# Four graph layers on one core: the adjacency test moved to the front, the first graphs listed anew, and seeds in place of a search

## The chip, the core and the metric

The kernel runs on one of the eight cores of a Trainium2 chip. The metric is the device time of one execution in microseconds. The time before is the median of three runs; one more execution was recorded by the hardware profiler, and the profile tells of that one.

## What is computed

There are 32 graphs of 512 nodes with 128 features in float32, and one adjacency matrix `adj` (512 x 512, zeros and ones, about 1.6% ones) that all graphs share. Four layers follow each other; each adds to `x` what it computes from `h = relu(layernorm(x))`:

```python
# layer 0
x_h = elu(h @ Wi + bi)
e = sigmoid(a_tgt[:, :, None] + a_src[:, None, :] + be) * (adj + 0.005 * (1 - (adj != 0)))
recv = elu(concat([einsum('bij,bjh->bih', e, x_h), x_h * sum(e, -1)]) @ Wn + bn)
x += concat([recv, x_h]) @ Wm + bm
# layer 1: five steps of a gated unit; m = adj @ h stands for both message inputs
z, r = sigmoid(m @ w3 + ... + h @ u3), sigmoid(m @ w4 + ... + h @ u3)
h = (1 - z) * h + z * tanh(m @ w5 + ... + (r * h) @ u5)
# layer 2
x += adj @ (h @ W) + bias
# layer 3: h, adj @ h, adj^2 @ h and adj^3 @ h (the two adjacencies are the same), each times a weight
```

## The kernel before

**Tiles.** A graph is one tile of 128 partitions by 512. Four graphs share a group buffer `x`. All other values live in numbered buffers: 36 of kind `f` (128x512 float32 in SBUF), 8 banks of PSUM of kind `b`, small ones for statistics (`s`), DRAM scratch (`m`, `d`). Layers 1 to 3 multiply by the adjacency in a rounded float32 type with a high and a low part (`r`), against the transposed adjacency (`A_r`), its column-shuffled form (`AQ`) and its square (`AA`).

**Order of the work.** No loop runs on the chip. Python code declares every operation with an engine, an estimated duration, a due time and its operands (`op`, line 63). The class `Plan` then plays the operations against those durations and writes one fixed order of instructions for each engine (`order`, line 124): of the operations that are ready, the one with the smallest due time goes first. An operation marked `two` excludes another such operation at the same time; by default all of GpSimd's operations are marked, and the VectorE operations with two inputs in SBUF. Where the plan finds TensorE without work before its time `FILL` (50), it inserts a matmul of ones into a spare bank, whose result nobody reads (line 348). The chip's engines run their lists in order and wait for each other by semaphores; the planned times are not on the chip.

**Two arms.** The kernel does not assume that the adjacency holds only zeros and ones. VectorE counts the other entries (line 561), TensorE sums the counts (line 582), VectorE writes the number to `other` (line 587), and every engine reads it and branches (lines 1069 and 1070). The arm `binary`, which these inputs take, uses the rounded type; the other arm is in float32. The part before the branch is planned up to time `BRANCH` (18), and each arm from there. Instructions that are listed later than that time stand behind the branch on their engine. For the arm `binary`, the function `searched_order` (line 221) shifts due times at random while the kernel is built, 240 times, and keeps the order whose planned end is earliest.

**The start.** SP issues the loads: `x` of graphs 0 and 1, the weight `Wi` and bias, the four blocks of `adj` (`A_nat`), `x` of graph 2, further weights. TensorE transposes the adjacency (line 570); ACT copies the result to `A_r` (line 572) and scales it by 200 (line 574), and VectorE makes from both the mask (1 where the entry is 0, 200 where it is 1; line 575). GpSimd copies the untransposed blocks to the rounded type (line 849) for the square.

**The layers' lines.** Layernorm (line 515): statistics on VectorE (lines 524 to 527), the power -1/2 on GpSimd (line 529), a shift on VectorE (line 533), then scale, shift and Relu on ACT (line 538); for the first `FIRST` (2) graphs the normalisation is on VectorE instead (line 544), the Relu is in the copy after the transpose (line 615), and the Relu of the first elu is on VectorE (line 600 in place of 603). Layer 0: projection (line 492, used for all products with one weight), scores (lines 634 to 641), tanh of the pair sums (line 686), times the mask (line 689), aggregation (line 697), row sums (lines 705 and 714, from graph 3 on by accumulating DMAs of GpSimd, line 721), output (line 744). Layer 1: adjacency products (line 913), rounding (lines 883 and 887), copies (lines 481 and 925). Graphs from the third on are turned by VectorE's 32x32 transpose and two DMAs through DRAM (line 433 and its DMAs at lines 435 to 474). Layer 3: lines 988 and 997, and the result at line 1015. Weights of the later layers are loaded behind the branch, summed on VectorE (line 800) and transposed (line 802).

Of the kernel before, what the change touches and what calls it, by code (L numbers as in the profile page):

```python
# [17 lines left out]
P = 128  # L18
# [4 lines left out]

class Val:
# [11 lines left out]
class Op:  # L36
    def __init__(self, eng, us, result, emit, two, keep):
        self.eng, self.us, self.result, self.emit, self.two, self.keep = eng, us, result, emit, two, keep
        self.before, self.after, self.vals, self.takes = set(), [], [], []
        self.ready, self.begun = 0.0, False  # L40


class Plan:
# [7 lines left out]
    def __init__(self, slots, ahead, last):  # L51
        self.ahead, self.last, self.ops, self.vals = ahead, last, [], {}
        self.free = {k: [(0.0, i) for i in range(n)] for k, n in slots.items()}
        self.until = dict.fromkeys(self.RESULT, 0.0)
        self.shared, self.now = 0.0, 0.0
        self.careful = 0.0
        self.slack = 0.0
        self.pieces = {}
        self.cold = 4.5
        self.fill = 0.0  # L60
        self.idle = None

# [61 lines left out]
    def order(self, end=None):  # L124

        left = [o for o in self.ops if not o.begun]
        for o in reversed(left):
            o.chain = o.us + max([o.margin, *(o.result + a.chain for a in o.after)])
            if end is None:
                o.due = min(o.due, self.last - o.chain)  # L130
        by_due, oldest = sorted(left, key=lambda o: o.due), 0
# [14 lines left out]
        def begins(o, now):  # L146
            if o.due > by_due[oldest].due + self.ahead:
                return False
            if o.two and self.shared > now:
                return False  # L150
            keep = 0 if o is by_due[oldest] else o.keep
            if any(v.added and self.clean(now) is None for v in o.takes):
                return False
            return all(
                len(self.free[v.kind]) > keep and self.free[v.kind][keep][0] <= now
                for v in o.takes
            )

        while events:
# [3 lines left out]
            for e in self.until:  # L163
                while coming[e] and coming[e][0][0] <= now:
                    _, i, o = heapq.heappop(coming[e])
                    heapq.heappush(ready[e], (o.due, i, o))
# [11 lines left out]
                if o is not None and now < self.careful and any(  # L178
                    c.due < o.due and t < now + 0.3 * o.us for t, _, c in coming[e]
                ):  # L180
                    heapq.heappush(ready[e], (o.due, index[o], o))
                    o = None
# [9 lines left out]
                while oldest + 1 < len(by_due) and by_due[oldest].begun:  # L192
                    oldest += 1
# [27 lines left out]
    def searched_order(self, until, rounds):  # L221


        ops = [o for o in self.ops if not o.begun]
        early, rng, asked = [o for o in ops if o.due < until], random.Random(3), self.state()

        def listed(due):
            self.back_to(asked)
            for o, d in zip(early, due):
                o.due = d  # L230
            return self.order()

        best, first = None, [o.due for o in early]
        due = first
        for _ in range(rounds):
            try:
                listed(due)
                end = max(o.start + o.us for o in ops)
                if best is None or end <= best[0]:
                    best = end, due  # L240
            except AssertionError:
                pass
            due = [*best[1]]
            if rng.random() < 0.5:
                start, width = rng.uniform(15, until), rng.uniform(2, 15)
                shift, eng = rng.gauss(0, 4), rng.choice(["PE", "ACT", "DVE", None, None])
                varied = {i: shift for i, o in enumerate(early)
                          if start <= first[i] < start + width and eng in (None, o.eng)}
            else:
                n = max(1, int(len(early) * rng.uniform(0.01, 0.1)))  # L250
                varied = {i: rng.gauss(0, 4) for i in rng.sample(range(len(early)), n)}
            for i, shift in varied.items():
                due[i] += shift
        return listed(best[1])


@with_exitstack
def tile_four_graph_layers(
# [35 lines left out]
    PACE, FIRST_PACE, LAST_PACE = 56.0, 14.0, 30.0  # L294
    BRANCH, FILL = 18.0, 50.0
    MARGIN = 10.0
    FIRST = 2

    T_MM, T_TR, T_NARROW, T_PASS = 0.86, 0.44, 0.224, 0.23
    T_VEC, T_COPY, T_ACT, T_DMA = 0.61, 0.5, 0.6, 0.45  # L300
# [82 lines left out]
    load_graph(0, -9, 2.5)  # L383
    load_graph(1, -9, 2.9)
    Wi_sb = load_const(Wi, [P, P], "Wi_sb", -9)
    bi_sb = load_column(bi, "bi_sb", -9)
    A_nat = [Val("f") for _ in range(NC)]
    for v in A_nat:
        v.left += 1
    for ic in range(NC):  # L390
        load(A_nat[ic], adj[ts(ic, P), :], -8, 0.48, result=3.9 + 0.2 * ic)
    load_graph(2, -8, 4.8)
# [12 lines left out]
    def scaled(v, factor, name, due):  # L405
        t = const(name, [P, 1])
        op("POOL", 0.4, due, lambda: nc.gpsimd.tensor_scalar(
            at(t), at(v), factor, None, op0=ALU.mult), [v], [t])
        return t
# [105 lines left out]
    def layernorm(b, due, relu=True, earliest=0.0):  # L515
# [6 lines left out]
        def moments():  # L522
# [5 lines left out]
        op("DVE", 1.3, due, moments, [X[b]], [s], earliest=earliest)  # L528
        op("POOL", 1.35, due, lambda: nc.gpsimd.tensor_tensor(  # L529
            stat(SCALE), stat(VAR), at(neg_half), op=ALU.pow), [s, neg_half], [s])  # L530
# [16 lines left out]
        if relu:  # L547
            op("ACT", 1.56, due, scale, [X[b], s], [h])
        else:
            op("DVE", 0.9, due, normed, [X[b], s], [h])  # L550
# [5 lines left out]
    A_r, mask = const("A_r", [P, NC, N], F32R), const("mask", [P, NC, N])  # L556
    other = const("other", [1, 1], I32)
    n_odd = const("n_odd", [P, NC])
    for ic in range(NC):
        odd = Val("f")  # L560
        op("DVE", 0.7, 9, lambda ic=ic, odd=odd: nc.vector.scalar_tensor_tensor(
# [3 lines left out]
    for jc in range(NC):  # L565
        pt, z = Val("b"), Val("f")
        pt.pieces = True
        def turn(jc=jc, pt=pt):
# [3 lines left out]
        op("ACT", T_COPY, 22, lambda jc=jc, pt=pt: nc.scalar.copy(at(A_r)[:, jc, :], at(pt)),  # L572
           [pt], [A_r])
        op("ACT", T_COPY, 9 + jc, lambda z=z, pt=pt: nc.scalar.mul(at(z), at(pt), 1 / ALPHA), [pt], [z])
        op("DVE", T_VEC, 9 + jc, lambda jc=jc, z=z, pt=pt: nc.vector.scalar_tensor_tensor(
            at(mask)[:, jc, :], at(pt), 0.0, at(z), op0=ALU.is_equal, op1=ALU.add),
            [pt, z], [mask])
# [8 lines left out]
    op("PE", 0.3, 9, count, [n_odd, ones], [p_odd])  # L586
    op("DVE", 0.2, 9, lambda: nc.vector.tensor_copy(at(other), at(p_odd)[:1, :1]),
# [23 lines left out]
    def layer0(b, h, due):  # L611
        KEEP = 12
        if b < G:
            pt, hT = transposed(h, due), Val("f")
            op("ACT", T_COPY, due, lambda pt=pt: nc.scalar.activation(
                at(hT), at(pt), AF.Relu if b < FIRST else AF.Copy), [pt], [hT])
        else:
            hT = turned_back(h, due)
            due += 6
# [59 lines left out]
        else:  # L679
            op("DVE", 0.1, d, turn, [ends], [flip])  # L680
            op("SP", T_DMA, d, gather, [flip], [row], result=2.6)
            op("SP", T_DMA, d, read, [row], [tgt], keep=KEEP, result=5.0)
        es = []
# [17 lines left out]
        if b < 2:  # L701
# [54 lines left out]
    def first_layer(b):  # L756
        h = layernorm(b, begin(b), relu=b >= FIRST, earliest=begin(b) - 12.0 if b < G else 0.0)
        layer0(b, h, begin(b))

    for b in range(G):  # L760
        first_layer(b)

# [11 lines left out]
    def arm(binary):  # L774
        with ExitStack() as stack:
# [5 lines left out]
            issue(plan.searched_order(130.0, 240) if binary else plan.order())  # L781

    def list_rest(binary, pool):
        n = 21 if binary else 16
# [22 lines left out]
        def gate_bias(w, u, name, due, factor):  # L807
            w, u = load_column(w, f"{name}w", due), load_column(u, f"{name}u", due)
            op("POOL", 0.4, due, lambda: nc.gpsimd.tensor_tensor(
                at(w), at(w), at(u), op=ALU.add), [w, u], [w])  # L810
            if factor != 1.0:
                op("POOL", 0.4, due, lambda: nc.gpsimd.tensor_scalar(
# [13 lines left out]
        for half in range(2):  # L826
# [11 lines left out]
            for k in range(4):  # L838
                op("POOL", 0.4, 110, lambda k=k, t=t, outs=outs: fold(k, t, outs), [t], [V[k]])


        for v in A_nat:
            v.left -= 1
        if binary:
            adjT = A_r
            adj2T = Val(tile=pool.tile([P, NC, N], F32R, tag="AA", name="AA"))
            nat = [Val("r") for _ in range(NC)]
            for kc in range(NC):
                op("POOL", 1.1, 24, lambda kc=kc: nc.gpsimd.tensor_copy(
                    at(nat[kc]), at(A_nat[kc])), [A_nat[kc]], [nat[kc]])  # L850
# [11 lines left out]
        else:  # L862
            adjT = Val(tile=pool.tile([P, NC, N], F32, tag="AT", name="AT"))
            for jc in range(NC):
                pt = Val("b")
                pt.pieces = True
                def turn(jc=jc, pt=pt):
                    for ic in range(NC):
                        nc.tensor.transpose(
                            at(pt)[:, ts(ic, P)], at(A_nat[ic])[:, ts(jc, P)], at(ident)  # L870
                        )
                op("PE", T_TR, 22, turn, [*A_nat, ident], [pt])
                op("ACT", T_COPY, 22, lambda jc=jc, pt=pt: nc.scalar.copy(
# [21 lines left out]
        op("POOL", 0.5, 34, lambda: nc.gpsimd.tensor_copy(  # L895
# [150 lines left out]
        for g in range(NG):  # L1046
            bs = range(g * G, (g + 1) * G)
            hT, uT = [], []
            for b in bs:
                if g:  # L1050
                    load_graph(b, max(begin(b) - 40, 4 + b))
                    first_layer(b)
# [61 lines left out]
```

## Time and profile before

| | us |
|---|---|
| median of three runs (1616.61 to 1618.88) | 1618.13 |
| profiled execution | 1619.53 |
| its span | 1617.7 |
| TensorE busy | 1604.9 |
| VectorE busy | 1407.0 |
| ScalarE (ACT) busy | 1128.7 |
| GpSimd (POOL) busy | 247.8 |

The span reaches from the first to the last instruction of the program; the execution's own time is 1.8 us more. PE is TensorE's matmul row and PEld its weight loads, which overlap it; DVE is VectorE. Float32 matmuls leave two records each. Where a row ends in `<-ENGINE`, it names what ended the idle time before it.

### The profile page before, as it was taken

What the parts mean: (1) busy time and instruction counts of PE and PEld (TensorE: products, weight loads), DVE (VectorE), ACT (ScalarE), POOL (GpSimd) and SP (SyncE); (2) the same over time, 40 slices, a digit from 0 to 9 for tenths busy, and PEclk for the clock granted to TensorE, in tenths of its full rate; (3) what the DMA queues carried; (4) which work ended last, traced back from release to release, by engine and by line L of the source; (5) the groups of instructions that cost most, each with busy time, mean ns of one, the idle gap of its engine ahead of it and who ended that gap; (6) DMA issues with size and microseconds to landing.
All of it is one profiled execution on the core that took longest, in us unless ns stands there. A gap on an engine that the chain in (4) does not pass through costs nothing.

```text
span 1617.7 us, 21058 instructions
## 1 busy us (share of the span) xinstructions
PE 1604.9 (99%) x6391; PEld 1032.3 (64%) x6391; DVE 1407.0 (87%) x3312; ACT 1128.7 (70%) x2133; POOL 247.8 (15%) x244
## 2 busy tenths in 40 slices
PE   9999999999999999999999999999999999999998
PEld 7655555666666666666666666666666666656687
DVE  7888999999998889889989889888999988888862
ACT  5876777877776676767776768777778766675652
POOL 3221001201111111111111121111111101100110
PEclk9999999999999999999999999999999999999999
DMA  3263444445443455434455444454355444323221
GB/s 95 79 145 105 124 137 124 108 113 152 125 130 105 112 137 138 127 103 125 117 136 132 123 107 123 131 144 131 101 143 136 131 101 122 104 92 98 85 59 48
DMA packets 284921, 188.00 MB, mean 116 GB/s; under 512 B 77312, under 2 KB 237952, under 8 KB 284800
## 3 DMA queue, kind: packets, MB, share of 16 engines
q1 hardware_dynamic: 270688, 162.98, 33.8%
q0 software_dynamic: 12528, 22.81, 8.7%
q8 instruction: 52, 0.85, 0.2%
q10 hardware_dynamic: 1584, 0.79, 0.2%
q14 instruction: 69, 0.57, 0.1%
HBM read 82.78 MB, written 73.33 MB: 97 GB/s over the span
## 4 chain that ended last, share of the span: by engine, by line
PE 97%; DVE 1%; ACT 1%; DMA 0%; issue 0%; DVEq 0%
PE b L492 45%; PE b L913 25%; PE b L988 7%; PE b L697 7%; PE b L744 4%; PE b L997 3%; PE b L976 2%; PE b L634 2%; PE b L348 1%; PE b L731 1%; DMA f<-m 0%; ACT f L538 0%; PE b L855 0%; ACT f L497 0%; DVE f L689 0%
## 5 line engine op out<-in xcount | busy, mean ns | idle before, releaser
L481 ACT COPY f<-b 128x512 f32<-128x512 f32 x388 | 223.6, 585 | 169.7 <-PE b L913 124.8
L529 POOL TENSOR_TENSOR s<-s,nhalf 128x4 f32<-128x4 f32 x128 | 159.5, 1247 | 943.7 <-DVE s L527 887.8
L913 PE MATMUL b<-AQ,r 128*128 128x512 f32 x1024 | 299.8, 435 | 0.0
L913 PEld LDWEIGHTS b<-AQ,r 128*128 128x128 f32 x1024 | 192.0, 188 | 85.9 <-issue 42.8
L938 DVE TENSOR_TENSOR f<-f,b 128x512 f32<-128x512 f32 x320 | 213.9, 679 | 28.3 <-PE b L492 22.6
L433 DVE STREAM_TRANSPOSE f<-f 128x512 f32<-128x512 f32 x246 | 207.1, 849 | 26.6 <-ACT f L538 26.0
L913 PE MATMUL b<-A_r,r 128*128 128x512 f32 x768 | 218.6, 427 | 2.0 <-DVE r L887 2.0
L538 ACT ACTIVATE f<-x,s 128x128 f32<-128x128 f32 x504 | 206.4, 485 | 14.3 <-DVE s L533 13.8
L497 ACT ACTIVATE f<-f,b4w 128x512 f32<-128x512 f32 x160 | 115.6, 723 | 118.9 <-DVE f L938 118.5
L913 PEld LDWEIGHTS b<-A_r,r 128*128 128x128 f32 x768 | 143.7, 188 | 60.7 <-issue 21.5
L492 PE MATMUL b<-f,u3T 128*128 128x512 f32 x320 | 163.4, 593 | 4.2 <-DMA f<-m 2.4
L887 DVE TENSOR_TENSOR r<-f,r 128x512 fp32r<-128x512 f32 x224 | 152.9, 685 | 16.4 <-ACT r L883 16.1
L492 PE MATMUL b<-f,u5T 128*128 128x512 f32 x320 | 163.2, 592 | 0.3 <-DVE f L945 0.3
L492 PE MATMUL b<-f,w3T 128*128 128x512 f32 x320 | 163.1, 592 | 0.0
L492 PE MATMUL b<-f,w5T 128*128 128x512 f32 x320 | 162.9, 592 | 0.0
L492 PE MATMUL b<-f,w4T 128*128 128x512 f32 x320 | 162.8, 592 | 0.0
L497 ACT ACTIVATE f<-b,b5w 128x512 f32<-128x512 f32 x160 | 109.6, 685 | 53.2 <-PE b L492 52.2
L883 ACT CAST r<-f 128x512 fp32r<-128x512 f32 x224 | 137.1, 618 | 12.1 <-DMA f<-m 11.0
L721 POOL DMA_DIRECT2D f<-f x87 | 77.6, 892 | 378.2 <-DMA f<-f 44.1
L497 ACT ACTIVATE f<-f,b3w 128x512 f32<-128x512 f32 x160 | 115.1, 721 | 27.1 <-DVE f L938 24.7
L955 DVE TENSOR_TENSOR f<-f,f 128x512 f32<-128x512 f32 x160 | 109.5, 685 | 26.3 <-ACT f L497 25.8
L988 PEld LDWEIGHTS b<-V,f 128*128 128x128 f32 x1024 | 122.8, 192 | 14.9 <-issue 12.7
(115 smaller groups left out, 2386.5 us busy)
## 6 DMA issues: line engine op xcount, KB each, us to landing
m<-f SPq DMA_DIRECT2D x246, 256.0 KB, 2.1
f<-m SPq DMA_DIRECT2D x186, 256.0 KB, 2.9
f<-f POOLq DMA_DIRECT2D x87, 256.0 KB, 3.7
f<-m SPq DMA_DIRECT2D x240, 64.0 KB, 2.4
x<-in_x_dram SPq DMA_DIRECT2D x32, 256.0 KB, 3.3
f<-f SPq DMA_DIRECT2D x29, 256.0 KB, 2.4
f<-d SPq DMA_DIRECT2D x28, 256.0 KB, 5.0
out_dram<-x SPq DMA_DIRECT2D x28, 256.0 KB, 2.5
```

Of the source, the lines that this page charges most:

```text
L433: op("DVE", us, due, lambda: nc.vector.transpose(view_out(at(blocks)), view_in(at(src))), [src], [blocks])
L481: op("ACT", us, due, lambda: nc.scalar.copy(at(t), at(src)), [src], [t])
L492: nc.tensor.matmul(to, at(w), of, start=start, stop=stop)
L497: op("ACT", us, due, lambda: nc.scalar.activation(at(dst), at(src), AF.Tanh, bias=at(bias), scale=scale), [src, bias], [dst])
L529: op("POOL", 1.35, due, lambda: nc.gpsimd.tensor_tensor(stat(SCALE), stat(VAR), at(neg_half), op=ALU.pow), [s, neg_half], [s])
L538: nc.scalar.activation(at(h)[:, ts(c, P)], at(X[b])[:, c, :], AF.Relu, bias=stat(SHIFT)[:, c : c + 1], scale=stat(SCALE)[:, c : c + 1],)
L697: op("PE", T_MM, d, lambda jc=jc: nc.tensor.matmul(at(pn), at(msg)[:, ts(jc, P)], at(es[jc]), start=jc == 0, stop=False), [msg, es[jc]], [pn])
L883: op("ACT", T_COPY, due, lambda: nc.scalar.copy(part(hi), whole()), [src], [hi], keep=1)
L887: op("DVE", T_VEC, due, lambda: nc.vector.tensor_tensor(part(lo), whole(), part(hi).bitcast(F32), op=ALU.subtract), [src, hi], [lo], two=two)
L913: nc.tensor.matmul(at(pa), at(part)[:, ts(jc, P)], view(at(columns)[:, jc, :]), start=jc == n == 0, stop=jc == NC - 1 and n == PARTS - 1,)
L938: op("DVE", T_VEC, d, lambda: nc.vector.tensor_tensor(at(s), at(u), at(pg), op=ALU.add), [u, pg], [s])
L988: nc.tensor.matmul(at(pz)[:, ts(i, D)], at(t[i])[:, ts(ic, P)], at(V[k]), start=i == n == 0, stop=last and i == G - 1 and n == len(terms) - 1,
```

## The change

- **The adjacency test first.** The four blocks of `adj` are loaded behind `x` of graph 0, ahead of `Wi`; the test's due times become -1, so that it stands ahead of other early work. `BRANCH` goes from 18 to 10. Layer 0 of the first four graphs is cut in two functions: `scored` is declared ahead of the branch, `aggregated` in the arms.
- **Mask and adjacency.** In the arm `binary` the mask is written by one ACT instruction per block, 1 + 199 times the transposed entry, in place of a scaling on ACT and an operation on VectorE. `A_r` is gone: GpSimd makes the transposed adjacency `AT` from the mask by a comparison (mask > 2), in place of four copies on ACT.
- **First graphs.** `FIRST` goes from 2 to 4, so graphs 2 and 3 also have their normalisation and first Relu on VectorE; `FIRST_PACE`, the spacing of the first graphs' due times, from 14 to 10.
- **Planner.** The power on GpSimd is no longer marked `two`, and durations are set anew (moments 1.26, power 1.2, normalisation 1.03 and others). The search is gone: 19 seeds, written in the file, each add one random set of shifts to due times below 130. The order is written in two parts, up to planned time 250 and from there.
- `ONES = 0` adds a branch of code that no graph takes.

Line numbers in the text up to the prediction are those of the kernel before.

```diff
+HEAD, TAIL = 250.0, 1500.0
+HEAD_NUDGES = (4000001, 4000006, 4000008, 4000034, 4000054, 4000088, 4000124, 4000206, 4000298, 4000710, 4000778,
+    4000852, 4001301, 4001728, 4002027, 4002029, 4002137, 4002150, 4002536)
+TAIL_NUDGES = ()
...
-            if end is None:
+            if self.complete:
                 o.due = min(o.due, self.last - o.chain)
-        by_due, oldest = sorted(left, key=lambda o: o.due), 0
+            o.turn = o.due + o.shift
+        by_turn, oldest = sorted(left, key=lambda o: o.turn), 0
...
-    def searched_order(self, until, rounds):
-
-
-        ops = [o for o in self.ops if not o.begun]
-        early, rng, asked = [o for o in ops if o.due < until], random.Random(3), self.state()
-
-        def listed(due):
-            self.back_to(asked)
-            for o, d in zip(early, due):
-                o.due = d
-            return self.order()
-
-        best, first = None, [o.due for o in early]
-        due = first
-        for _ in range(rounds):
-            try:
-                listed(due)
-                end = max(o.start + o.us for o in ops)
-                if best is None or end <= best[0]:
-                    best = end, due
-            except AssertionError:
-                pass
-            due = [*best[1]]
+    def nudge(self, low, high, seeds):
+
+        ops = [o for o in self.ops if not o.begun and low <= o.due < high]
+        dues = [o.due for o in ops]
+        for seed in seeds:
...
+                for o, due in zip(ops, dues):
+                    if start <= due < start + width and eng in (None, o.eng):
+                        o.shift += shift
...
+                for i in rng.sample(range(len(ops)), n):
+                    ops[i].shift += rng.gauss(0, 4)
...
-    PACE, FIRST_PACE, LAST_PACE = 56.0, 14.0, 30.0
-    BRANCH, FILL = 18.0, 50.0
+    PACE, FIRST_PACE, LAST_PACE = 56.0, 10.0, 30.0
+    BRANCH, FILL = 10.0, 50.0
     MARGIN = 10.0
-    FIRST = 2
+    FIRST = 4
+    ONES = 0
...
-    T_VEC, T_COPY, T_ACT, T_DMA = 0.61, 0.5, 0.6, 0.45
+    T_VEC, T_COPY, T_ACT, T_DMA = 0.605, 0.5, 0.6, 0.45
...
-    load_graph(0, -9, 2.5)
-    load_graph(1, -9, 2.9)
+    load_graph(0, -10, 2.5)
+    A_nat = [Val("f") for _ in range(NC)]
+    for ic, v in enumerate(A_nat):
+        load(v, adj[ts(ic, P), :], -9.5, 0.48, result=2.7 + 0.25 * ic)
     Wi_sb = load_const(Wi, [P, P], "Wi_sb", -9)
     bi_sb = load_column(bi, "bi_sb", -9)
-    A_nat = [Val("f") for _ in range(NC)]
-    for v in A_nat:
-        v.left += 1
-    for ic in range(NC):
-        load(A_nat[ic], adj[ts(ic, P), :], -8, 0.48, result=3.9 + 0.2 * ic)
-    load_graph(2, -8, 4.8)
+    load_graph(1, -8.5, 3.2)
+    load_graph(2, -8, 4.0)
...
-        op("DVE", 1.3, due, moments, [X[b]], [s], earliest=earliest)
-        op("POOL", 1.35, due, lambda: nc.gpsimd.tensor_tensor(
-            stat(SCALE), stat(VAR), at(neg_half), op=ALU.pow), [s, neg_half], [s])
+        op("DVE", 1.26, due, moments, [X[b]], [s], earliest=earliest)
+        op("POOL", 1.2, due, lambda: nc.gpsimd.tensor_tensor(
+            stat(SCALE), stat(VAR), at(neg_half), op=ALU.pow), [s, neg_half], [s], two=False)
...
-            op("DVE", 0.9, due, normed, [X[b], s], [h])
+            op("DVE", 1.03, due, normed, [X[b], s], [h])
...
-    A_r, mask = const("A_r", [P, NC, N], F32R), const("mask", [P, NC, N])
+    mask = const("mask", [P, NC, N])
+    plan.vals[mask] = True
...
-        op("DVE", 0.7, 9, lambda ic=ic, odd=odd: nc.vector.scalar_tensor_tensor(
+        op("DVE", 0.62, -1, lambda ic=ic, odd=odd: nc.vector.scalar_tensor_tensor(
...
-    for jc in range(NC):
-        pt, z = Val("b"), Val("f")
+    A_turned = [Val("b") for _ in range(NC)]
+    for jc, pt in enumerate(A_turned):
         pt.pieces = True
         def turn(jc=jc, pt=pt):
             for ic in range(NC):
                 nc.tensor.transpose(at(pt)[:, ts(ic, P)], at(A_nat[ic])[:, ts(jc, P)], at(ident))
         op("PE", T_TR, 8, turn, [*A_nat, ident], [pt])
-        op("ACT", T_COPY, 22, lambda jc=jc, pt=pt: nc.scalar.copy(at(A_r)[:, jc, :], at(pt)),
-           [pt], [A_r])
-        op("ACT", T_COPY, 9 + jc, lambda z=z, pt=pt: nc.scalar.mul(at(z), at(pt), 1 / ALPHA), [pt], [z])
-        op("DVE", T_VEC, 9 + jc, lambda jc=jc, z=z, pt=pt: nc.vector.scalar_tensor_tensor(
-            at(mask)[:, jc, :], at(pt), 0.0, at(z), op0=ALU.is_equal, op1=ALU.add),
-            [pt, z], [mask])
...
-    op("PE", 0.3, 9, count, [n_odd, ones], [p_odd])
-    op("DVE", 0.2, 9, lambda: nc.vector.tensor_copy(at(other), at(p_odd)[:1, :1]),
+    op("PE", 0.3, -1, count, [n_odd, ones], [p_odd])
+    op("DVE", 0.2, -1, lambda: nc.vector.tensor_copy(at(other), at(p_odd)[:1, :1]),
...
+    def first_turned(b, h, due):
+        pt, hT = transposed(h, due), Val("f")
+        op("ACT", T_COPY, due, lambda: nc.scalar.activation(
+            at(hT), at(pt), AF.Relu if b < FIRST else AF.Copy), [pt], [hT])
+        return hT
+
+    def scored(b, hT, due):
...
+        return xhT, msg, ends, tgt, like_tgt, of_tgt
+
+    def aggregated(b, begun, due):
+        KEEP = 12
+        if b >= G:
+            due += 6
+        pace = 0.6 if b < FIRST else 1.0
+        xhT, msg, ends, tgt, like_tgt, of_tgt = begun
+        d = due + 20 * pace
...
-    def first_layer(b):
+    def entry(b):
         h = layernorm(b, begin(b), relu=b >= FIRST, earliest=begin(b) - 12.0 if b < G else 0.0)
-        layer0(b, h, begin(b))
-
-    for b in range(G):
-        first_layer(b)
-
+        return first_turned(b, h, begin(b)) if b < G else turned_back(h, begin(b))
+
+    begun = [scored(b, entry(b), begin(b)) for b in range(G)]
+    crossing = [*A_turned, *A_nat, *(v for x in begun for v in x[:4])]
+    for v in crossing:
+        v.left += 1
...
-            issue(plan.searched_order(130.0, 240) if binary else plan.order())
+            plan.complete = True
+            if not binary:
+                issue(plan.order())
+                return
+            plan.nudge(0.0, 130.0, HEAD_NUDGES)
+            order = plan.order(end=HEAD)
+            plan.nudge(TAIL, 2000.0, TAIL_NUDGES)
+            issue(order + plan.order())
 
     def list_rest(binary, pool):
+        for v in crossing:
+            v.left -= 1
+        for jc, pt in enumerate(A_turned):
+            def masked(jc=jc, pt=pt):
+                nc.scalar.activation(at(mask)[:, jc, :], at(pt), AF.Identity,
+                                     bias=at(ones)[:, :1], scale=1 / ALPHA - 1)
+            if binary:
+                op("ACT", T_COPY, 9 + jc, masked, [pt, ones], [mask])
+                continue
+            z = Val("f")
+            op("ACT", T_COPY, 9 + jc, lambda z=z, pt=pt: nc.scalar.mul(at(z), at(pt), 1 / ALPHA), [pt], [z])
+            op("DVE", T_VEC, 9 + jc, lambda jc=jc, z=z, pt=pt: nc.vector.scalar_tensor_tensor(
+                at(mask)[:, jc, :], at(pt), 0.0, at(z), op0=ALU.is_equal, op1=ALU.add),
+                [pt, z], [mask])
+        for b in range(G):
+            aggregated(b, begun[b], begin(b))
...
-            adjT = A_r
+            adjT = Val(tile=pool.tile([P, NC, N], F32R, tag="AT", name="AT"))
+            for jc in range(NC):
+                op("POOL", 0.7, 22, lambda jc=jc: nc.gpsimd.tensor_scalar(
+                    at(adjT)[:, jc, :], at(mask)[:, jc, :], 2.0, None, op0=ALU.is_gt), [mask], [adjT])
...
-                op("POOL", 1.1, 24, lambda kc=kc: nc.gpsimd.tensor_copy(
-                    at(nat[kc]), at(A_nat[kc])), [A_nat[kc]], [nat[kc]])
+                op("POOL", 0.62, 24, lambda kc=kc: nc.gpsimd.tensor_copy(
+                    at(nat[kc]), at(A_nat[kc])), [A_nat[kc]], [nat[kc]], earliest=26.0)
...
-                    first_layer(b)
+                    aggregated(b, scored(b, entry(b), begin(b)), begin(b))
...
```

## The prediction

> **What bounds the kernel now.** I read the busy shares first, then the chain that ended last, then busy time by stretches (cut where the activity changes), then TensorE's own waits.
>
> ```profile
> PE 1604.9 (99%) x6391; PEld 1032.3 (64%) x6391; DVE 1407.0 (87%) x3312; ACT 1128.7 (70%) x2133; POOL 247.8 (15%) x244
> ```
>
> TensorE is busy 1604.9 of 1617.7 us, and the chain is 97% PE. But "busy" includes matmuls that compute nothing: line 348 multiplies ones into a spare PSUM bank wherever the planner, up to its time 50, found TensorE without work. The stretches (PE, PEld, DVE, ACT, POOL) show where something is left to win:
>
> ```profile
> 0.00:20.00 20.00, 18.65 (x132) 17.07 (x133) 13.93 (x55) 10.80 (x21) 6.33 (x17) 1.00 0.45 127
> 20.00:50.00 30.00, 29.99 (x162) 21.53 (x162) 22.65 (x72) 21.53 (x48) 7.44 (x12) 1.00 0.26 77
> 50.00:110.00 60.00, 55.39 (x210) 32.71 (x210) 52.30 (x118) 48.72 (x95) 16.57 (x18) 1.00 0.45 113
> 110.00:160.00 50.00, 50.00 (x170) 28.86 (x169) 43.48 (x97) 31.70 (x55) 8.70 (x9) 1.00 0.41 105
> 160.00:860.00 700.00, 699.24 (x2650) 438.74 (x2649) 637.73 (x1492) 510.90 (x967) 106.31 (x96) 1.00 0.46 124
> 860.00:1560.00 700.00, 700.00 (x2745) 447.81 (x2744) 616.78 (x1426) 485.43 (x910) 98.22 (x90) 1.00 0.43 117
> 1560.00:1613.49 53.49, 51.61 (x332) 45.58 (x330) 20.12 (x55) 19.59 (x42) 4.18 (x4) 1.00 0.16 45
> ```
>
> From 110 to 1560 TensorE idles 0.8 us in all, while VectorE (91% and 88% in the long stretches) has some room. So this kernel's time is the real matmul work plus fillers plus idle gaps, and all of the last two lie in the first 110 us and the last 60. TensorE's waits of the first 160 us, the filler row, and one row of the tail:
>
> ```profile
> PE b L492 <- DMA f<-m: 2.4, 1, 2.4
> PE b L492 <- ACT f L925: 1.8, 1, 1.8
> PE b L348 <- DVE ones L343: 1.0, 1, 1.0
> PE b L634 <- DVE f L607: 0.3, 1, 0.3
> ...
> L348 PE MATMUL b<-ones x138: 272/275/580, 1.0 to 49.2; 128*128 128x128 f32 x138
> ...
> 1589.03 2.11 PE L913 MATMUL b<-A_r,r 128*128 128x512 f32 x8 [1.05 <-DVE r L887]
> ```
>
> A float32 matmul leaves two records, so 138 records are 69 fillers. Nine of them ran from 44.59 to 46.60, 0.223 us each; the first block of 21 ran from 1.04 to 8.45, 0.353 each, slow at its start.
>
> **The change part by part.**
>
> *TensorE's work.* In the built instruction order of the taken arm, every kind of real matmul and transpose has the same count before and after; only the names of tiles change. The fillers go from 69 to 44: 15 instead of 21 ahead of the first transpose, 29 instead of 48 later. The six lost at the end of the first block are at the faster rate, so 25 x 0.223 = 5.6 us go, if no wait stands in their place. The time comes from this, from idle, or not at all: nothing else shortens TensorE's list.
>
> *What lets the planner drop them: the elementwise engines.* ACT is the tight one: from 37 to 70 it is busy 29.9 of 33 us, and the 1.8 us wait at 68 is for its copy at line 925. The change takes from ACT four casts of the adjacency (line 572, 2.2 us for four), the normalisation of graphs 2 and 3 (line 538, two times 1.65), and their two Relus (line 603, spaced 0.57): 2.2 + 3.3 + 1.1 = 6.6 us. The four scalings at line 574 become four mask writes of the same shape, taken at the same 0.5 us spacing: nothing. VectorE loses four mask operations (2.6) and two shifts (0.3), and gains two normalisations (line 544, 1.1 per graph) and two Relus (line 600, 0.74): +0.8 us. GpSimd gains four 128x512 comparisons that make the adjacency from the mask. The nearest row is its cast of that size: four in 2.81 us, 0.70 each. No row shows the comparison, so I bound it by 0.6 and twice 0.70, and take 0.70.
>
> *Does the work fit?* I walk the new order. SP issues x of graph 0 at 0.73, then the four adjacency blocks from 1.2 to 2.6 (spacing 0.47); at the 3.7 us that such loads take to land they are there by 6.3. TensorE's 15 fillers end near 7.0 and its 16 transposes near 8.9. VectorE: statistics from 3.8, tests and normalisation 3 x 0.61 + 1.1 + 0.61, so the count is whole near 8.6, and after graph 1's statistics the flag is written near 10.1 (before: 16.67). Input projection and weights issued behind the adjacency (Wi near 3.1, x of graph 1 near 4.1) land by 7.8 and are wanted at 9.4 and 8.6: they cost nothing; graph 0's own work is the cover.
>
> *The branch.* Its row before:
>
> ```profile
> SPq L1069 <- DVE other L587: 7.8, 1, 7.8
> L1069 SPq TENSOR_LOAD <-other x1: 470/470/470, 16.7 to 16.7; - x1
> L1069 PEldq TENSOR_LOAD <-other x1: 492/492/492, 17.8 to 17.8; - x1
> ```
>
> SP idled 7.8 us and issued its next load at 17.65, 0.98 us after the flag. TensorE read the flag at 17.8, long after it was set, behind queued fillers. Now all engines reach it as it is written: ACT with graph 0's exponential behind it, GpSimd with two powers, TensorE with 12 fillers, SP with x and weights. Each resumes near 10.9. Bounds for TensorE: nothing (one filler before it covers) and 1.0; I take 0.4. SP gains 6.7 us on the weight loads (17.65 to 10.9). Graph 0's features are ready a little later than before (near 16.5 against 15.05), because ACT stood at the branch. The first weight sum on VectorE stands ahead of that step and needs a load issued near 12.3 (landing 3.1 later, 15.4): it costs 0 to 0.8, I take 0.3.
>
> *The milestone.* Ahead of the first aggregation matmul (line 697) the new list holds about 9.6 us of real work and all 44 fillers: 7.0 + 9.6 + 29 x 0.223 + 0.7 of waits, near 23.5. Before, at 23.5 TensorE has done 23.5 - 1.35 idle - 7.4 - 24 x 0.223 = 9.4 of real work, and 24 fillers (5.4 us) still come. From there to layer 1's first adjacency product the new list has 27.9 us of matmuls: 19 float32 products of 0.86 spacing, 16 of the rounded kind and 16 of line 744's at 0.22, ten of 0.25 with the score columns, and 17 transposes of 0.11. VectorE's queue to the operand of that product is 22.6 us of work from 23.9 on, ACT's 17.6 from 22.4: slack of about 5 and 11 us where the old list had a 0.2 us wait on VectorE. So near 51.4 the new list has done 37.5 of real work; the old one had done 34.4 at 53.98, where its first such product starts (18.1 of fillers and 1.5 of idle taken off), and reached 37.5 near 57.1: 5.7 us ahead.
>
> *Later waits of the head.* With ACT ahead, I take the 1.8, and 0.4 of small waits, as gone. The 2.4 us at 101 is a turn through DRAM (line 435 and its return): its order is new, so it could go, stay or grow; I keep it. Comparisons at the upper bound push the last adjacency block to about 18.6, against its use at 18.9: nothing, or 1 us in the range.
>
> *Powers beside VectorE.* The planner no longer holds back two-input VectorE work during a power. The row first:
>
> ```profile
> 53.48 1.31 POOL L529 TENSOR_TENSOR s<-s,nhalf 128x4 f32<-128x4 f32 x1 [11.94 <-DVE s L527]
> 53.84 2.09 DVE L689 SCALAR_TENSOR_TENSOR f<-f,mask 128x512 f32<-128x512 f32 x3
> ```
>
> Inside a power of 1.31 VectorE began a two-input operation and ran three in 2.09, 0.70 spacing against 0.61: at most 0.2 us lost per power. [...] The row decides: nothing.
>
> *The tail.* Before, the last graph's transposes go straight into its product, which waits 1.05 us. The new order puts four matmuls of line 997 (0.9 us) between. I take 0.9. The last store, 4.2 us after the last VectorE row, stays.
>
> *Sum.* -5.6 fillers, -2.2 waits of the head, -0.9 tail, +0.4 branch (the weight sum's 0.3 is absorbed by the following fillers or slack): -8.3. The profiled execution took 1619.5 around its span of 1617.7; the median 1618.1 is 1.4 below it. The parts carry over: 1618.1 - 8.3 = 1609.8 us.
>
> **The rivals.** (1) *Waits take the fillers' places.* The planner knows no flag read, and where its durations are short TensorE stalls. For: the 4.6 us of waits after 50 show that it misses some. Against: up to 50 the old list shows 1.35 us of idle in all. If half of the fillers come back as waits (2.8) and the 2.2 stay: -8.3 + 5.0, 1614.8. (2) *The DRAM turn goes too*, with the rest of the tail and middle: -8.3 - 2.4 - 1.0, 1606.4; the floor, since no more idle is there. [...] (4) *It doesn't do what it says*: overlap already happened before the change, as the row above shows, so that part may be void; the first graphs' part cannot be, as the order shows it.
>
> **How the numbers follow.** Forecast 0.62, (1) 0.19, (2) 0.14, (3) 0.05. What a measurement tells from no change is about 0.2%, 3.2 us: faster means below 1614.9. Half of (1) falls inside: same 0.08; slower 0.05, the lock; faster 0.87. Range: from (2) with 1 us of uncertainty, 1605.4, to the unknown costs (comparison 1.0, branch 0.6, weight sum 0.5, a larger DRAM wait 2) on the forecast, 1613.9.
>
> **What would show it.** Right: 88 filler records, no new wait above 0.5 us before 50 except at the branch, the flag written near 10, first aggregation near 23.5, the L925 wait gone, the last product's wait near 0.1, real matmul time unchanged. Wrong: waits on VectorE or GpSimd's adjacency tiles between 15 and 50 that sum to over 3 us; VectorE rows beside powers longer than 1 us; idle in 160 to 1560 well above 0.8; another DRAM wait of several us before 110.

## The result and the profile after

| | before | after |
|---|---|---|
| median, five runs each | 1618.88 us | 1610.65 us |
| profiled execution / its span | 1619.53 / 1617.7 | 1609.89 / 1608.1 |
| TensorE busy | 1604.9 | 1599.2 |
| TensorE idle in the span | 12.8 | 8.9 |

The ratio is 0.9951, with a 95% interval of 0.9937 to 0.9966: 8.2 us faster in the medians. The two profiled spans differ by 9.6 us, because the profiled run of before lies 0.65 us above its median and that of after, the fastest of its five, 0.76 below. The split below is made on the spans. From here on a line number is that of the kernel whose profile is shown; in the changed kernel line 339 is the filler, 560 the transposes of the adjacency, 825 the transposes of later weights, 481 all products with one weight.

The busy shares of after:

```profile
PE 1599.2 (99%) x6341; PEld 1026.2 (64%) x6341; DVE 1405.8 (87%) x3316; ACT 1120.9 (70%) x2119; POOL 248.0 (15%) x248
```

Busy time by stretches (stretch, its length, then PE, PEld, DVE, ACT and POOL with instruction counts, granted clock, DMA share, GB/s), then TensorE's waits of the first 160 us and the filler row:

```profile
0.00:20.00 20.00, 17.27 (x119) 14.84 (x120) 13.84 (x64) 9.08 (x15) 11.31 (x20) 1.00 0.65 179
20.00:50.00 30.00, 29.81 (x132) 18.58 (x131) 28.84 (x77) 23.87 (x53) 10.57 (x13) 1.00 0.13 41
50.00:110.00 60.00, 60.00 (x228) 36.20 (x227) 51.39 (x119) 44.85 (x88) 17.06 (x21) 1.00 0.51 126
...
160.00:860.00 700.00, 699.35 (x2657) 439.28 (x2657) 637.73 (x1500) 506.41 (x959) 104.43 (x97) 1.00 0.46 123
...
PE b L825 <- DMA b4u<-in_L_gnn_u_b_dram: 1.1, 1, 1.1
PE b L339 <- DVE ones L334: 1.0, 1, 1.0
PE b L560 <- DMA f<-in_adj_dram: 0.6, 2, 0.3
PE b L481 <- ACT f L597: 0.2, 1, 0.2
...
L339 PE MATMUL b<-ones x88: 273/275/582, 1.0 to 24.7; 128*128 128x128 f32 x88
```

The fillers end at 24.7 us, where they ended at 49.2 before. TensorE idles 2.9 us up to 50, against 1.4: it waits for the adjacency and, 1.1 us at line 825, for the first weight behind the branch. (The row names another load, of a bias; the weight's own load is named at its PEld record, with a wait of 1.89 us.) From 50 to 110 it idles not at all, where it idled 4.6. So of the 9.6 us, 5.7 is busy time, 4.6 is waits after 50 us, 0.75 is the tail (0.9 expected for one wait there); 1.6 was given back in the first 50 us; small changes make up the rest. The busy time is the fillers': their own rows add up to 20.0 us before and 13.1 after. That is 6.9 less, so the real matmuls, 6253 records in both, took about 1 us longer; why is not shown.

### The profile page after: what moved, and what is told of

Read it like the earlier page. It is cut to its first block, busy times and chain, and to the rows that moved or that the text cites. A ratio compares the mean times of both kernels' runs of the same rounds, so it can differ in the third digit from the quotient of the medians.

```text
span 1608.1 us, 20921 instructions
## 1 busy us (share of the span) xinstructions
PE 1599.2 (99%) x6341; PEld 1026.2 (64%) x6341; DVE 1405.8 (87%) x3316; ACT 1120.9 (70%) x2119; POOL 248.0 (15%) x248
## 4 chain that ended last, share of the span: by engine, by line
PE 96%; DVE 1%; DMA 1%; ACT 1%; SPq 0%; issue 0%; POOL 0%; DVEq 0%; ACTq 0%; POOLq 0%
PE b L481 45%; PE b L932 25%; PE b L1007 7%; PE b L691 7%; PE b L1016 4%; PE b L742 4%; PE b L995 2%; PE b L619 2%; PE b L729 1%; DMA f<-m 1%; DMA f<-in_adj_dram 0%; SPq L352 0%; ACT f L527 0%; PE b L882 0%; PE b L410 0%
## 5 line engine op out<-in xcount | busy, mean ns | idle before, releaser
L518 POOL TENSOR_TENSOR s<-s,nhalf 128x4 f32<-128x4 f32 x128 | 154.4, 1206 | 975.9 <-DVE s L516 791.4
L932 PE MATMUL b<-AQ,r 128*128 128x512 f32 x1024 | 304.2, 439 | 0.0
L957 DVE TENSOR_TENSOR f<-f,b 128x512 f32<-128x512 f32 x320 | 213.3, 678 | 29.9 <-PE b L481 23.8
L932 PE MATMUL b<-AT,r 128*128 128x512 f32 x768 | 220.3, 429 | 0.0
L932 PEld LDWEIGHTS b<-AT,r 128*128 128x128 f32 x768 | 144.0, 188 | 58.8 <-issue 25.3
```

What stands on the lines that cost most here:

```text
L518: op("POOL", 1.2, due, lambda: nc.gpsimd.tensor_tensor(stat(SCALE), stat(VAR), at(neg_half), op=ALU.pow), [s, neg_half], [s], two=False)
L932: nc.tensor.matmul(at(pa), at(part)[:, ts(jc, P)], view(at(columns)[:, jc, :]), start=jc == n == 0, stop=jc == NC - 1 and n == PARTS - 1,)
L957: op("DVE", T_VEC, d, lambda: nc.vector.tensor_tensor(at(s), at(u), at(pg), op=ALU.add), [u, pg], [s])
```

## Experiments

All kernels were timed in five or more rounds beside the kernel before. Medians and ratios are given below; a ratio's interval is about 0.0013 to either side, 2 us, and half of that for the kernels with many rounds. All have the same real matmuls; "fillers" are counted in the instruction order. Each searched order is one draw; other seeds for the same kernel were tried once only (the last two rows, 1.1 us apart), so the scatter of draws is not well known.

| kernel | fillers | median us | ratio to before |
|---|---|---|---|
| before (240 random steps in its build) | 69 | 1617.5 to 1618.9 | 1 |
| before, no search | 63 | 1625.92 | 1.0044 (1.0030 to 1.0059) |
| before, 1000 steps | 62 | 1613.98 | 0.9973 (0.9962 to 0.9983) |
| after, no seeds | 47 | 1616.68 | 0.9991 (0.9984 to 0.9997) |
| after, other seeds from 1000 steps | 52 | 1611.72 | 0.9956 (0.9942 to 0.9970) |
| after, its 19 seeds | 44 | 1610.65 | 0.9951 (0.9937 to 0.9966) |

**Are the fillers themselves the delay?** Both orders were kept, and the fillers left out when the lists were written:

```diff
             for o in operations:
-                o.emit()
+                if o is not plan.idle:
+                    o.emit()
```

Of the kernel before:

> The kernel before with its order unchanged, but the 69 filler matmuls are left out of TensorE's list. Theory A (fillers only stand where TensorE would have waited for operands; the gain of the change comes from operands that are ready sooner): TensorE waits in the same places, the time stays within 1.5 us of the kernel before, and idle of the first 50 us grows from 1.4 to about 15 us. Rival B (the fillers themselves hold TensorE back, so that dropping 25 of them was the gain): the time falls by 5 us or more, up to 17 (69 fillers of 0.25), without any other part of the change. Rival C (fillers hold the clock up): real matmuls of the first 50 us run slower, and it ends over 3 us slower.

It took 1619.32 us, ratio 1.0003 (0.9995 to 1.0011). Of the changed kernel:

> The changed kernel with its order unchanged, but its 44 fillers left out. Theory A: within 1.5 us of the changed kernel (1610.6). Rival B: faster by 4 to 10 us. Rival C: slower by over 3 us, with transposes and projections of the first 20 us at twice their time.

It took 1611.85 us, ratio 0.9962 (0.9949 to 0.9976), 1.2 us above the changed kernel and so within what theory A allowed. Rival B falls: without any of the 69 fillers the old order is no faster. They stand where TensorE would have waited. The 5.7 us of busy time that went are therefore waits in disguise, and by this reading the gain is that operands come sooner. Rival C is half right, as stretches of the first of these two kernels show (stretch, length, PE busy with count, granted clock, DMA share, GB/s), with one row of its work:

```profile
16.99:20.40 3.41, 1.51 (x8) 1.00 0.25 55
20.40:23.82 3.42, 3.42 (x6) 0.50 0.85 236
44.30:47.71 3.41, 1.33 (x9) 1.00 0.32 110
47.71:51.12 3.41, 3.41 (x19) 0.50 0.66 216
...
19.79 5.37 PE L697 MATMUL b<-f,f 128*128 128x512 f32 x8 [1.90 <-DVE f L689]
```

Twice, after a stretch with waits, the clock was granted at half for 3.41 us. Four products took 5.37 us where they took 3.60 in the kernel before, and already at 9.59 us two records of line 492 took 1.91 us where they took 1.02. So in the old order the fillers did hold the clock up: with them it was 1.00 in all four of these stretches. The changed kernel without its 44 kept 1.00 up to 60 us. In the old order it cost little in the end. With no fillers ahead of them the four products began 0.92 us earlier (19.79 against 20.71), and at line 634's scores the two kernels are in step again (27.86 and 27.93). The second halving left layer 1's first adjacency product 0.6 us later (54.59 against 53.98).

**Seeds, or the rebuilt start?** The changed kernel with `HEAD_NUDGES = ()`:

> The changed kernel without its 19 seeds: due times are not shifted. Its list has 47 fillers against 44. If the rebuilt start makes the gain and the seeds little: 0.7 us for three fillers and 0 to 3 us of waits after 50 us, so 1611 to 1614. If the seeds make the gain, it stands near 1618.

1616.68 us: neither range was met. Its trace says where the 6 us went (line by line, the time an instruction group starts and takes, and in brackets the idle time before it):

```profile
1339.71 1.91 PE L480 MATMUL b<-f,u3T 128*128 128x512 f32 x2 [3.25 <-DMA f<-m]
1341.41 4.55 PE L690 MATMUL b<-f,f 128*128 128x512 f32 x8
...
1336.50:1339.91 3.41, 0.20 (x1) 1.00 0.85 275
1339.91:1343.33 3.42, 3.42 (x5) 0.50 0.60 168
```

TensorE waits 3.25 us for a turn through DRAM at 1336 us, far from the start that the seeds shift, and the clock is then granted at half (0.50) for 3.41 us, which by estimate, half of that time, costs another 1.7: eight records in 4.55 where they took 3.60 in the kernel before. That is 5 of the 6. The planner continues one order to the end, so a shift before 130 us can change which operations meet at 1336; that the seeds did so by anything but chance is not shown.

The kernel before, with its search replaced by seeds from 1000 steps (`searched_order(130.0, 240)` becomes a replay of nine seeds):

> The kernel before, but its own 240 random steps are replaced by a search of 1000 steps of the kind the change replays (due times below 130 shifted, a step kept where the planned end is earlier; nine kept). 62 fillers against 69. Theory S (a longer search alone is the gain): near the changed kernel, 1612 or less. Theory R (the rebuilt start is what lets the search find more): 7 fillers fewer, 1.6 us, and 0 to 2 us of waits: 1615 to 1618.

1613.98 us: faster than theory R allowed, slower than theory S wanted. Another, longer search alone gives 4 us on the old start. That its length did it, and not a lucky draw, is not tested. The same search on the changed kernel:

> The changed kernel with other seeds: the same search of 1000 steps as in the run of the kernel before with 1000 steps (five kept). 52 fillers against 44. Theory R: the gain is in the structure, so another search finds most of it: 8 fillers, 1.8 us, more than the changed kernel, 1611 to 1613.5. Theory S or luck (the 19 seeds are a lucky draw for the chip): near the kernel without seeds, 1616 to 1618.

1611.72 us, as theory R said. And the old start with `plan.order()` in place of its search:

> The kernel before without any search: due times as declared. 63 fillers against 69. If the search is what a start of this kind lives on: slower than the kernel before by 2 to 6 us, in waits and not in fillers (fillers alone say 1.3 us faster). If the 240 steps brought nothing on the chip: within 1 us of it, or faster.

1625.92 us, 8.4 us slower than the kernel before and more than the 2 to 6 expected. Fewer fillers did not help. TensorE idles 16.0 us of its span of 1624.5, 3.2 more than before, and is busy 3.6 us longer although six fillers are gone. Of its TensorE waits and stretches:

```profile
PE b L421 <- ACT f L538: 2.6, 1, 2.6
PE b L697 <- DVE f L689: 2.5, 1, 2.5
PE b L913 <- DVE r L887: 1.7, 2, 1.1
...
52.68:56.09 3.41, 2.98 (x7) 0.50 0.00 0
1592.09:1595.50 3.41, 2.60 (x6) 0.50 0.02 5
1595.50:1598.92 3.42, 3.42 (x15) 0.50 0.00 0
```

Each of the two waits of over 2.5 us comes with half the clock (0.50), for 10.24 us in all; by estimate that cost up to half of it, about 5 us.

So the search and the rebuilt start overlap in what they gain. Without a search the rebuilt start is worth 1625.9 - 1616.7 = 9.2 us, of which, by the same estimate, up to 3.4 is the difference in time at half clock (10.24 us against 3.41). With 1000 steps on both sides it is worth 1614.0 - 1611.7 = 2.3 us; the intervals of the ratios, 0.9962 to 0.9983 and 0.9942 to 0.9970, overlap, and each side is one draw. What speaks for a part of the start's own is that all seven searched orders of the rebuilt start, those below included, took 1609.5 to 1612.8 us, against 1614.0. By the ratios, of about 8 us some 4.4 go with the other search on the old start, some 2.8 with the rebuilt start, and the last 0.8 is too little to be told from another draw. The changed kernel also writes its order in two parts and adds its shifts apart from the due times, where the kernels with 1000 steps shift the due times themselves; that difference is not tested.

**Powers beside VectorE.** The kernel without seeds, with the powers kept apart again behind the branch (`two=None` there):

> As the kernel without seeds, but behind the branch the planner again keeps GpSimd's powers apart from two-input VectorE work, as the kernel before did. 55 fillers against 47. If the planner's licence to overlap is worth something: 8 fillers of 0.22, 1.8 us slower than without it, or a little more. [...] If the powers overlapped anyway, the same within 1 us in spite of the fillers.

1615.35 us, ratio 0.9984 (0.9978 to 0.9991): no slower in spite of 55 fillers against 47, and without the wait at 1336 (an accident of the order). With seeds from 1000 steps:

> The changed kernel with GpSimd's powers kept apart from two-input VectorE work behind the branch, the same search (eight kept). 47 fillers against 52. If the licence to overlap brings nothing, 5 fillers fewer: 1610 to 1611.7. If the overlap is worth something that the plan shows late: slower than 1612.5, by waits of TensorE or a longer layernorm.

1610.58 us, ratio 0.9952 (0.9938 to 0.9965): no slower than with the licence (1611.72). The licence to overlap brings nothing that these runs can tell.

**ACT's relief.** `FIRST = 4` back to `2`, seeds from 1000 steps:

> The changed kernel with graphs 2 and 3 normalised on ACT again (FIRST = 2), and the same search of 1000 steps (17 kept). 54 fillers against 52. If ACT's relief (4.4 us of it here) carries the gain: ACT busy again over 90% between 37 and 70 us, waits of TensorE on ACT after 50, 2 to 4 us slower than the structure with FIRST = 4. If not: within 1 us of it.

1612.09 us, ratio 0.9958 (0.9944 to 0.9971), as with 4 (1611.72). Its stretch from 50 to 110:

```profile
50.00:110.00 60.00, 60.00 (x217) 35.38 (x217) 53.63 (x124) 48.92 (x95) 16.44 (x21) 1.00 0.46 120
```

ACT is as busy there (48.92) as before the change (48.72), and TensorE idles not at all. Relief of ACT did not remove those waits.

**The adjacency from GpSimd.** ACT copies the transposed adjacency from PSUM, as before:

```diff
-                op("POOL", 0.7, 22, lambda jc=jc: nc.gpsimd.tensor_scalar(
-                    at(adjT)[:, jc, :], at(mask)[:, jc, :], 2.0, None, op0=ALU.is_gt), [mask], [adjT])
+                op("ACT", T_COPY, 22, lambda jc=jc: nc.scalar.copy(
+                    at(adjT)[:, jc, :], at(A_turned[jc])), [A_turned[jc]], [adjT])
```

> The changed kernel with the transposed adjacency copied by ACT from PSUM as before, instead of GpSimd's comparison of 1.48 us each, and the same search (eight kept). 49 fillers against 52. If the slow comparison holds the early work up: waits in the first 25 us fall by 1 us or more and it is 0.5 to 2 us faster. If the 2 us on ACT matter more: 1 to 2 us slower.

1609.83 us, ratio 0.9949 (0.9935 to 0.9962): 1.9 us under the structure with GpSimd's comparison; the intervals of the two ratios overlap. The move to GpSimd is not what gains.

**The early branch.** `BRANCH = 18.0`, seeds from 1000 steps:

> The changed kernel with the branch back at planned time 18 in place of 10, other seeds by the same search of 1000 steps (six kept). 62 fillers against 52 with the branch at 10. If the early branch is worth what the fillers say (the later weights, the mask and the GpSimd work all stand behind it): 10 x 0.22, 2.2 us, and some waits, 2 to 4 us slower than 1611.7. If the branch doesn't matter: within 1 us of it.

1612.82 us, ratio 0.9963 (0.9949 to 0.9978): 1.1 us more than at 10. TensorE has 10 fillers more and, in the profiled run, which is the slowest of the five, one wait of 2.2 us at 110 to 160 behind VectorE. The sign is as expected; the size is not told from nothing.

**A version meant to beat both.** The ACT copy, `x` of graphs 4 to 7 held until planned time 16 (`earliest=16.0` in their load, so weights go first behind the branch), and ten seeds from 2500 steps:

> A version meant to beat both: the changed kernel with the transposed adjacency copied by ACT, the x loads of graphs 4 to 7 held until planned time 16 so that the weights stand ahead of them behind the branch, and seeds from a search of 2500 steps (ten kept). 47 fillers. If the weight waits near 17 us (1.1 on TensorE, 1.2 on VectorE) and the slow comparisons cost time: 1607 to 1609.5. If the start is bound by the loads ahead of the branch and by VectorE: no better than the ACT copy alone, 1609 to 1611.

1609.54 us, ratio 0.9945 (0.9931 to 0.9959): the fastest of all, and not told apart from the changed kernel. The weight wait went from 1.1 to 0.5 us, but the adjacency now held TensorE for 1.5.

Taken out one at a time, the licence, ACT's relief, GpSimd's comparison and the early branch moved the time by -1.9 to +1.1 us; none of these is told apart from no change. The other edits of the start (the load order, the cut of layer 0, the mask by ACT, the new durations) were not taken out singly, nor were two parts of ACT's relief together. Which edit carries the rebuilt start's share stays open.

## Why the prediction was right, point by point

- **Fillers, 5.6 us:** TensorE's busy time fell by 5.7. The count of 44 held, and so did the real matmuls' (6253 records), but the size hides two parts: the fillers' own rows fell by 6.9, and the real matmuls took about 1 us longer. The two kernels without fillers add that this is displaced waiting.
- **Waits after 50, 2.2 us: mis-sized.** 4.6 went. I kept the 2.4 us turn through DRAM; it is gone too, as rival (2) had it.
- **The start, 0.4 us: mis-sized.** 1.6 us of new idle, and with the 1.1 us at line 825 the sign "no new wait above 0.5 us before 50" failed. Three things were late. The adjacency blocks took 4.7 us to land, not 3.7, so TensorE waited 0.6 in its transposes. The flag came at 10.55 (10.1 in the sum) and SP issued again at 11.68 (10.9). The weight loads were issued at 13.10 and 13.65 (12.3), and their first uses were at 17.73 on VectorE and 17.95 on TensorE, where the sum had 15.4. First aggregation: 25.25 against 23.5 (whose four terms add up to 23.8); first adjacency product: 53.5 against 51.4. Against my 57.1 for the old list, after is then 3.6 us ahead, not 5.7. The idle that follows in the kernel before (4.4 us from there to 110, and 0.75 in the tail) brings that to 8.8 of the 9.6, so 57.1 was itself somewhat early.
- **The branch's row** is as told for four engines: SP, ACT, GpSimd and TensorE read the flag at 10.7 us, as it is written, where TensorE read it at 17.8 before. VectorE read it 1.1 us later, behind its statistics.

```profile
L571 DVE CAST other<-b x1: 140/140/140, 10.6 to 10.6; 1x1 int32<-1x1 f32 x1
L1088 PEldq TENSOR_LOAD <-other x1: 490/490/490, 10.7 to 10.7; - x1
L1088 DVEq TENSOR_LOAD <-other x1: 545/545/545, 11.8 to 11.8; - x1
...
L871 POOL TENSOR_SCALAR AT<-mask x4: 1482/1487/1522, 13.9 to 18.8; 128x512 fp32r<-128x512 f32 x4
```

- **GpSimd's comparison, 0.70 each (bound 1.4): wrong.** The last row: 1.48 each. The cast was the wrong neighbour, and its 0.70 was a mean that hid three of 0.61 and one of 1.14. The last block came at 20.3, where the upper bound had 18.6, and its product began at 20.34 with no wait on record: fillers stood ahead of it.
- **Powers beside VectorE: nothing.** The row held. In after, VectorE runs four two-input operations at their usual 0.60 spacing across a whole power, which itself takes 1.39 (1.00 at the shortest). At the row's 0.2 each, the 57 powers between 160 and 860 in the kernel before could have cost 11 us; 160 to 860 has the same 637.73 us of VectorE. The 0.05 for slower stood on VectorE being stopped for the whole of a power, which no run shows; what shows are those four operations in 2.49 us. Beside four casts of 128x512 VectorE's operations took 0.96 to 1.09 us (last rows):

```profile
33.59 2.49 DVE L683 SCALAR_TENSOR_TENSOR f<-f,mask 128x512 f32<-128x512 f32 x4
33.76 1.39 POOL L518 TENSOR_TENSOR s<-s,nhalf 128x4 f32<-128x4 f32 x1 [4.32 <-DVE s L516]
...
25.57 3.87 POOL L876 CAST r<-f 128x512 fp32r<-128x512 f32 x4
25.84 1.09 DVE L703 TENSOR_TENSOR f<-f,f 128x512 f32<-128x512 f32 x1
26.99 0.96 DVE L683 SCALAR_TENSOR_TENSOR f<-f,mask 128x512 f32<-128x512 f32 x1
```

- **The tail, 0.9 us:** 0.75. The wait of 1.05 before the last graph's product is gone, with line 1016 in between:

```profile
1576.46 1.17 PE L1016 MATMUL b<-r,AA 128*128 128x512 f32 x4
1577.47 1.99 PE L932 MATMUL b<-AT,r 128*128 128x512 f32 x8
```

- **The reason was not right.** I put ACT's relief behind the shorter list. Giving most of it back (4.4 of 6.6 us) changed nothing measurable. ACT's busy time did fall, by 7.8 us, and VectorE's by 1.2 where the sum had 0.8 more. The counts and places that the prediction read from the built order held; why the order is shorter is the rebuilt start and the seeds together, and the seeds' share was not in any step. The rival of waits in the fillers' places did happen (1.6 us), and was outweighed by the waits that went later.
- **That the number fits is in part luck.** On the spans the four terms measured 5.7, 4.6 and 0.75 gained and 1.6 lost, 9.4 us where the sum had 8.3: the waits were taken 2.4 too small and the start 1.2 too cheap. In the medians 1.4 us of this is not there, since the two profiled runs lie on opposite sides of theirs. Reading the built order gave the place and the sign of each term, not this agreement.

## What to carry to other kernels

Where TensorE bounds a kernel whose order is written ahead, read fillers as waits: compare their count in the two instruction orders, then check the stretches where idle stood. Before crediting the edits of such a kernel, give both versions the same search: here, in one order each, the edits were worth 9 us without one and 2 with one, and one wait far from the edit moved the sum by 5. Price an operation that no row shows by more than its nearest relative in shape (here 1.48 us against 0.61).

## What the runs showed of the hardware

- **Half the clock came behind stretches of 3.41 us with little TensorE work, and the length of one wait did not tell.** The rows above show the clock granted at half five times ahead of the last matmul, four times for 3.41 us and once for 6.83. The clock's records leave out the start: they begin at 6.56 us in the kernel before and at 4.88 in after, and from there to the last matmul it was 1.00 in both. The beginnings fit one grid: 20.40 and 47.71 in one trace lie 8 times 3.41 us apart, 52.68 and 1592.09 in another 451 times 3.413. Each stretch of this grid just ahead of a halving held 1.51 us of work or less: 0.20, 1.33 and 1.51 in the rows above, 1.31 twice in the old start without a search. In the one with 1.33 the two waits were of only 1.00 and 1.08 us. A stretch with 1.55 us of work was followed by the full clock in the kernel before (first rows below; it begins 28 times 3.413 us behind the first record), where the wait of 2.38 us lies across two stretches. With the branch at 18 the clock stayed at 1.00 from 110 to 160 us, where one wait was of 2.2. So the most work ahead of a half clock was 1.51 us in these rows, and the least ahead of the full one, in the kernel before, 1.55; the waits ahead of a half clock were of 1.00 to 3.25 us.
- **Casts on GpSimd and VectorE operations with two inputs in SBUF took longer beside each other.** In the kernel before, three casts of 128x512 with no such operation beside them took 0.61 us. One that began 0.01 us behind such an operation of VectorE took 1.14, 0.53 more, while VectorE took its usual 0.68 (last rows below). In after, beside four casts, VectorE's operations took 0.96 to 1.09 us and three of the casts 1.07; their ends alternate, each of VectorE's 0.54 us behind a cast's and 0.47 ahead of the next. What holds them up is not shown. Beside a power of 128x4, of 1.39 us, VectorE lost nothing in after: its operations kept their 0.60 spacing.

```profile
102.13:105.54 3.41, 1.55 (x8) 1.00 0.36 125
105.54:108.96 3.42, 3.42 (x20) 1.00 0.68 152
...
19.04 0.68 DVE L689 SCALAR_TENSOR_TENSOR f<-f,mask 128x512 f32<-128x512 f32 x1
19.05 1.14 POOL L849 CAST r<-f 128x512 fp32r<-128x512 f32 x1
```

- **A comparison of 128x512 on GpSimd took 1.48 us**, 2.4 times the 0.61 of those three casts.
